# Keys stored for both bands and loaded in one transfer a half; input tiles stored as one run a partition

## The chip, the cores and the metric

The kernel runs on one core of a Trainium2 chip. The metric is the device time of one execution in microseconds; the median of three runs stands for a kernel. A profiled execution supplies the trace: one execution, with its own time.

The core's engines are TensorE (PE, its weight loads PEld), VectorE (DVE), ScalarE (ACT) and GpSimd (POOL). SyncE (SP) here only issues DMA transfers. Each engine has its own in-order instruction stream, and semaphores tie them together. Transfers run on the core's 16 DMA engines.

## The reference

The input is 16 images of 3 x 512 x 512 values in float32. The kernel computes a tokenizer and one transformer layer:

```python
h = patches(x) @ W.T + b                      # 1024 tokens of 256, patches of 3*16*16 = 768
q, k, v = heads(layernorm(h) @ w_qkv)         # 8 heads of 32
k = sum_f a[f]*sin(f*k) + b[f]*cos(f*k)       # f = 1 .. 256, elementwise
h = h + (softmax(q k' * 32**-0.5) @ v) @ w_out + b_out
h = h + shared_mlp(n) + top_2_of_4_experts(n) # n = layernorm(h)
```

The sum of 256 sines and cosines for each element of k is the costly part. Sums are kept in float32.

## The kernel before

The work of an image is cut in two ways. Tokens, projections and networks go by half images (512 tokens). Keys and attention go by head pairs: 4 a image, 64 in all, numbered p.

**Input.** `load_x` (L496 to L505) loads one tile `x` of 128 tokens, 128 partitions x 6 x 128 values, on SP (L501). In HBM an image is laid out as 768 rows of 1024 tokens, so a partition's part of a tile is six pieces of 128 values. There are three buffers; a load is issued when the tile three before it has been used. `tokens` runs the matmuls `tok`.

**Keys.** The angles of k are written to HBM (`ud`, L623). `load_waves` (L971) fetches each row again, spread over partitions, into tiles `w`, eight buffers (two tiles a group g, eight groups a pair); `load_source` (L990) fetches `src` for the tiles `f`. GpSimd multiplies them by frequencies (`turn_waves`, L1026), ScalarE takes the sine (L1036), TensorE mixes (`mix`, `kan`, L1056), VectorE multiplies (L1070), and TensorE adds up (`add_up`, `red`, L1089). After four rounds of `red` a pair's 128 rows of 512 key values stand in PSUM.

`finish_keys` (L1102) splits them into a high part in float32r and the rest (`khi`, `klo`; L635, L636) and writes both to the HBM tensor `kd`, 128 rows of 512 values each (L1108). `stack_keys` (L1114) then fills the two tiles `k4[half]`, named `k` in the profile: 128 partitions x 2 x 512 values of which the first 64 partitions hold the high and low rows (32 each) and the other 64 the same again, so that high and low queries can be multiplied with both. It does this by two transfers of 64 partitions from the same source for each half (L1119), four a pair. Each `kd` transfer writes 256 KB, each `k` transfer loads 256 KB. `stack_queries` (L1136) does the like for queries.

**Attention.** `score` (`sT`, L1155) multiplies keys and queries, ScalarE takes exponentials (`es`, L1170), `weigh` (`av`, L1188) sums values and weights, and VectorE normalizes (L1212 on). Each pair has two attention rounds, over the two halves of the queries, eight scores each; the first four read `k4[0]`, the others `k4[1]`. A pair's keys may be loaded into `k4[half]` after the last score of the pair before that reads it.

**Order.** All loops over images, pairs and groups are unrolled by a planner in the kernel's own source. It keeps a modelled clock for each engine and a queue of steps with dependences (`put`), and lays the next step of SP, POOL, ACT or DVE by modelled readiness. TensorE's order isn't planned: it is a string written out by hand, `ORDER`, one letter a step. `transfer(took, issue)` moves the modelled DMA clock; its result goes into `done[...]`, from which the other steps' due times follow. So a changed number there can move instructions on the planned engines.

After the planned part the kernel checks a flag and, where the softmax sums were out of bounds, would run `general_path`, which this input doesn't reach. It has its own `load_x`.

Of the kernel before, what the change touches and what calls it, by code (L numbers as in the profile page):

```python
# [11 lines left out]
FP = mybir.dt.float32  # L12
# [6 lines left out]
P = 128  # L19
# [3 lines left out]
N = 1024  # L23
NT = N // P
PD = 768
NKC = PD // P
# [17 lines left out]
XT = 128  # L44
# [46 lines left out]
def plain_path(ctx: ExitStack, tc: tile.TileContext, a: dict, out: bass.AP, verdict: bass.AP):  # L91
# [9 lines left out]
    nc = tc.nc  # L101
    xT = a["xT"]
# [3 lines left out]
    def pool(name, bufs, space=None):  # L106
        kw = {} if space is None else {"space": space}
        return ctx.enter_context(tc.tile_pool(name=name, bufs=bufs, **kw))
# [6 lines left out]
    kdp = pool("kdp", 2, DRAM)  # L115
# [137 lines left out]
    k4 = [const.tile([P, 2, 520], FPR, tag=f"k4{i}", name=f"k4{i}") for i in range(2)]  # L253
# [16 lines left out]
    done = {}  # L270
# [8 lines left out]
    def put(engine, queue, cost, deps, key, action):  # L279

        queues[engine].setdefault(queue, []).append((cost, deps, key, action))
# [48 lines left out]
    def transfer(took, issue=0.0, ready=0.0):  # L330

        clock[SP] = max(clock[SP], ready) + issue
        now["dma"] = max(now["dma"], clock[SP]) + took
        return now["dma"] + LANDS
# [161 lines left out]
    def load_x(b, j):  # L496

        b, j = b + j // (N // XT), j % (N // XT)
        if b < B:
            t = xp.tile([P, NKC, XT], FP, tag="x", name="x")  # L500
            nc.sync.dma_start(  # L501
                out=t, in_=xT[b, :, ts(j, XT)].rearrange("(c p) n -> p c n", p=P)
            )
            chunks[b, j] = t
            done["x", b, j] = transfer(1.75, 0.6, clock[PE])  # L505
# [38 lines left out]
    def tokens(b, half):  # L544

        st = images[b]
        if b >= 3:
            yield "written", b - 3, half
        h = st["h", half] = hp.tile([P, 4, E], FP, tag="h", name="h")
        for t in range(4):  # L550
            j = 4 * half + t
            yield "x", b, j
            yield ANY
            ps = side_tile("tok")[:, 0:E]
            for c in range(NKC):
                matmul(
                    out=ps,
                    lhsT=chunks[b, j][:, c, :],
                    rhs=wt[:, c, :],
                    start=(c == 0),  # L560
                    stop=(c == NKC - 1),
                )
            del chunks[b, j]
            load_x(b, j + XBUFS)
            for action in deferred.pop(j + b * (N // XT), ()):
                action()
            yield DVE, 0.41
            nc.vector.tensor_add(h[:, t, :], ps, tokb)  # L568
        mark("tokens", b, half)
# [59 lines left out]
    def split(src, name):  # L629

        hi, lo = (
            rup.tile([P, 512], FPR, tag=tag, name=name + half)
            for tag, half in (("r", "hi"), ("u", "lo"))
        )
        nc.vector.tensor_copy(hi, src)  # L635
        nc.vector.tensor_sub(lo, src, hi.bitcast(FP))  # L636
        return hi.bitcast(FP), lo.bitcast(FP)
# [436 lines left out]
    rows_of_pair = {}  # L1074
# [27 lines left out]
    def finish_keys(p):  # L1102


        def action():
            kd = rows_of_pair["k", p] = kdp.tile([2, P, 512], FP, tag="kd", name="kd")
            for i, x in enumerate(split(rows_of_pair.pop(p), "k")):
                nc.sync.dma_start(out=kd[i], in_=x)  # L1108
            done["kd", p] = transfer(1.4, 1.1, done["keys", p])

        deps = [("red", 4 * p + 3)] + ([("k4", p - 2, 1)] if p > 1 else [])
        put(DVE, "keys", 1.41, deps, ("keys", p), action)

    def stack_keys(p, half):  # L1114

        def action():
            src = rows_of_pair["k", p].rearrange("i (d s h) n -> h (i d) s n", s=2, h=2)[half]
            for j in range(2):
                nc.sync.dma_start(out=k4[half].bitcast(FP)[ts(j, 64), :, 0:512], in_=src)  # L1119
            done["stacked", p, half] = transfer(1.9)  # L1120

        deps = [("kd", p)] + ([("score", 2 * p - 1, 4 * half + 3)] if p > 0 else [])
        put(SP, "keys", 0.8, deps, ("k4", p, half), action)
# [133 lines left out]
    for j in range(XBUFS):  # L1257
        load_x(0, j)
# [73 lines left out]
def general_path(  # L1332
# [33 lines left out]
    nc = tc.nc  # L1366
# [38 lines left out]
    for c in range(2):  # L1405
        for side in range(2):
            nc.sync.dma_start(
                out=wq[:, c, :, ds(64 * side, HD)],
                in_=w_qkv[ts(c, P), 0:E].rearrange(
                    "p (i s d) -> p i s d", s=2, d=HD  # L1410
                )[:, :, side, :],
# [44 lines left out]
    def load_x(b, j):  # L1456
        t = xp.tile([P, NKC, XT], FP, tag="x", name="x")
        nc.gpsimd.dma_start(
            out=t,
            in_=xT[ds(b, 1), :, ts(j, XT)].rearrange("o (c p) n -> p (o c) n", p=P),  # L1460
        )
        return t

# [33 lines left out]
    def stage_tokens(b):  # L1497

        h = hp.tile([P, NT, E], FP, tag="h", name="h")
        for g in range(2):  # L1500
            ps = big_tile("tok").rearrange("p (t e) -> p t e", e=E)
            for k in range(4):
                j, col = divmod((4 * g + k) * P, XT)
                if col == 0:
                    chunk = load_x(b, j)
                for c in range(NKC):
                    nc.tensor.matmul(
                        out=ps[:, k, :],
                        lhsT=chunk[:, c, ds(col, P)],
                        rhs=wt[:, c, :],  # L1510
                        start=(c == 0),
                        stop=(c == NKC - 1),
                    )
            nc.vector.tensor_add(
                h[:, ts(g, 4), :], ps, tokb.unsqueeze(1).to_broadcast([P, 4, E])
            )
# [397 lines left out]
def _patches(x):  # L1914

    b, c, hh, ww = x.shape
    p = 16
    t = x.reshape(b, c, hh // p, p, ww // p, p).transpose(0, 1, 3, 5, 2, 4)
    return np.ascontiguousarray(t.reshape(b, c * p * p, (hh // p) * (ww // p)))


def _kan_layout(kan_a, kan_b):
# [138 lines left out]
```

## Time and profile before

| | before |
|---|---|
| median of 3 runs, us | 3914.31 (3911.86 to 3915.78) |
| the profiled execution, us | 3913.84 |
| its span in the profile, us | 3912.3 |
| TensorE busy, us | 3811.7 |
| ScalarE busy, us | 3264.3 |
| GpSimd busy, us | 3197.1 |
| VectorE busy, us | 2525.4 |
| DMA traffic, MB | 916.53 |
| granted TensorE clock, mean | 0.994 |

The span runs from the first instruction to the last; the time of the execution has some 1.5 us around it. An engine's busy time leaves out waiting, branches and DMA issues. Matmuls overlap, so their ends are modelled. A line such as "POOL w L1026 <- DMA w<-ud: 273.0, 98, 9.6" reads: in front of GpSimd's instruction of line 1026 that writes `w`, the engine stood idle for 273.0 us in total, 98 times, 9.6 us at the longest, and each time the landing of a transfer from `ud` into `w` ended the wait. "SPq" is SP's queue of DMA issues. A packet is the piece of a transfer that one DMA engine moves at a time; here a piece is one contiguous run.

### The profile page before, as it was taken

What the parts mean: (1) busy time and instruction counts of PE and PEld (TensorE: products, weight loads), DVE (VectorE), ACT (ScalarE), POOL (GpSimd) and SP (SyncE); (2) the same over time, 40 slices, a digit from 0 to 9 for tenths busy, and PEclk for the clock granted to TensorE, in tenths of its full rate; (3) what the DMA queues carried; (4) which work ended last, traced back from release to release, by engine and by line L of the source; (5) the groups of instructions that cost most, each with busy time, mean ns of one, the idle gap of its engine ahead of it and who ended that gap; (6) DMA issues with size and microseconds to landing.
All of it is one profiled execution on the core that took longest, in us unless ns stands there. A gap on an engine that the chain in (4) does not pass through costs nothing.

```text
span 3912.3 us, 102935 instructions
## 1 busy us (share of the span) xinstructions
PE 3811.7 (97%) x40337; PEld 1949.1 (50%) x40337; DVE 2525.4 (65%) x4075; ACT 3264.3 (83%) x3939; POOL 3197.1 (82%) x2328
## 2 busy tenths in 40 slices
PE   7899999999999999999999999999999999999998
PEld 4334454554545555455454545545455554544444
DVE  4756757666675766757667575766767667576552
ACT  2788888888888888888888888888888888888983
POOL 3988879788788878879788788878879888888870
PEclk9999999999999999999999999999999999999999
DMA  7997968888788888878888788787878888778760
GB/s 231 283 255 213 278 197 248 256 230 259 214 260 231 233 262 228 259 218 257 243 236 260 211 255 249 225 255 222 267 214 252 258 226 265 223 231 254 213 179 21
DMA packets 589665, 916.53 MB, mean 234 GB/s; under 512 B 60877, under 2 KB 179573, under 8 KB 589173
## 3 DMA queue, kind: packets, MB, share of 16 engines
q1 hardware_dynamic: 588036, 909.40, 80.0%
q8 instruction: 321, 5.26, 0.6%
q14 instruction: 172, 1.40, 0.1%
q10 hardware_dynamic: 1136, 0.47, 0.0%
HBM read 758.64 MB, written 150.99 MB: 233 GB/s over the span
## 4 chain that ended last, share of the span: by engine, by line
PE 70%; ACT 9%; DMA 9%; POOL 4%; DVE 3%; issue 3%; SPq 1%; ACTq 0%; POOLq 0%; DVEq 0%
PE av L1188 17%; PE sT L1155 10%; PE kan L1056 9%; DMA w<-ud 6%; PE red L1089 4%; PE tok L319 4%; ACT w L1036 3%; PE e1p L319 3%; PE e3p L319 3%; PE tok L322 3%; POOL w L1026 2%; ACT f L1036 2%; PE e1p L322 2%; ACT es L1170 2%; PE s1p L319 2%
## 5 line engine op out<-in xcount | busy, mean ns | idle before, releaser
L1026 POOL TENSOR_TENSOR w<-w,lane 128x1024 int32<-128x1024 int32 x1024 | 1925.6, 1897 | 391.6 <-DMA w<-ud 273.0
L1170 ACT ACTIVATE es<-sT 128x1024 f32<-128x1024 f32 x1024 | 1014.9, 1022 | 340.9 <-PE sT L1155 296.8
L1036 ACT ACTIVATE w<-w 128x1024 f32<-128x1024 int32 x1024 | 1013.3, 1046 | 70.5 <-POOL w L1026 67.3
L1026 POOL TENSOR_TENSOR f<-f,lane 128x1024 int32<-128x1024 int32 x512 | 971.4, 1897 | 105.2 <-DVE f L1011 89.8
L1070 DVE TENSOR_TENSOR f<-kan,f 128x1024 f32<-128x1024 f32 x512 | 605.0, 1214 | 207.9 <-ACT f L1036 112.1
L1155 PE MATMUL sT<-q,k 128*128 128x512 f32 x2048 | 708.1, 455 | 22.0 <-ACT es L1170 12.3
L1011 DVE STREAM_SHUFFLE f<-src 128x1024 int32<-128x1024 int32 x512 | 683.1, 1373 | 0.4
L1188 PE MATMUL av<-es,v 128*32 128x256 f32 x8192 | 638.7, 383 | 14.8 <-ACT es L1170 12.3
L1188 PE MATMUL av<-es,ones 128*32 128x256 f32 x8192 | 631.0, 380 | 0.0
L1056 PE MATMUL kan<-w,coef 64*32 64x512 f32 x8192 | 542.3, 599 | 20.5 <-ACT w L1036 13.2
L1036 ACT ACTIVATE f<-f 128x1024 f32<-128x1024 int32 x512 | 518.9, 1045 | 4.2 <-POOL f L1026 4.2
L1155 PEld LDWEIGHTS sT<-q,k 128*128 128x128 f32 x2048 | 350.8, 189 | 316.8 <-issue 137.1
L1188 PEld LDWEIGHTS av<-es,v 128*32 128x32 f32 x8192 | 234.7, 109 | 356.2 <-issue 232.9
L1188 PEld LDWEIGHTS av<-es,ones 128*32 128x32 f32 x8192 | 267.1, 110 | 176.4 <-issue 1.4
L1212 DVE RECIPROCAL rc<-av 128x256 f32<-128x256 f32 x128 | 224.7, 1755 | 164.4 <-PE av L1188 164.3
L1056 PEld LDWEIGHTS kan<-w,coef 64*32 64x32 f32 x8192 | 129.3, 105 | 317.2 <-issue 127.3
L1089 PE MATMUL red<-f,pack 128*32 128x512 f32 x2048 | 271.6, 603 | 0.0
L319 PE MATMUL tok<-wt,x 128*128 128x256 f32 x768 | 182.6, 390 | 18.8 <-DMA x<-in_xT 11.1
L531 ACT ACTIVATE hn<-h,less,rstd 128x256 f32<-128x256 f32 x256 | 140.7, 591 | 52.4 <-POOL less L523 51.8
L1036 ACT ACT_TABLE_LOAD x128 | 164.2, 1283 | 17.8 <-DMA w<-ud 15.5
L322 PE MATMUL tok<-wt,x 128*32 128x256 f32 x3072 | 178.0, 380 | 1.0 <-DVE h L568 1.0
L319 PEld LDWEIGHTS tok<-wt,x 128*128 128x128 f32 x768 | 148.1, 195 | 54.9 <-issue 21.3
(148 smaller groups left out, 4264.5 us busy)
## 6 DMA issues: line engine op xcount, KB each, us to landing
w<-ud SPq DMA_DIRECT2D x2048, 256.0 KB
q<-qd SPq DMA_DIRECT2D x512, 128.0 KB
k<-kd SPq DMA_DIRECT2D x256, 256.0 KB
x<-in_xT SPq DMA_DIRECT2D x128, 384.0 KB
ud<-u SPq DMA_DIRECT2D x64, 512.0 KB
ud<-ui SPq DMA_DIRECT2D x64, 512.0 KB
src<-ud SPq DMA_DIRECT2D x512, 64.0 KB
qd<-qhi SPq DMA_DIRECT2D x64, 256.0 KB
```

Source lines behind the costliest of these rows:

```text
L319: nc.tensor.matmul(out=out, lhsT=lhsT, rhs=rhs, start=start, stop=stop)
L322: nc.tensor.matmul(out=out[ts(i, 32)], lhsT=lhsT[:, ts(i, 32)], rhs=rhs, start=start, stop=stop)
L1011: nc.vector.stream_shuffle(w, sources[g // 8].rearrange("p r n -> p (r n)"), [4 * (g % 8) + i // 8 for i in range(32)],)
L1026: nc.gpsimd.tensor_tensor(w, w, f.to_broadcast([P, N]), ALU.mult)
L1036: nc.scalar.activation(x, w, AF.Sin, scale=TURN * 2.0**-32)
L1056: nc.tensor.matmul(out=ps[ds(64 * j + 32 * blk, 32), ts(r, 512)], lhsT=coef[ts(r, 64)].rearrange("p e f j -> p (e f j)"), rhs=w[ts(r, 64), ...
L1070: nc.vector.tensor_mul(w, kan.pop(g), w)
L1089: nc.tensor.matmul(out=rows_of_pair[p][ts(2 * i + r, 32), :], lhsT=pack[:, ds(PACK0 - 16 * (k % 2) - 2 * (k // 2), 32)], rhs=prod[:, ts(r, ...
L1155: nc.tensor.matmul(out=ps[:, ts(s, 512)], lhsT=k4[kc // 4][:, s, ts(kc % 4, P)], rhs=q4[:, s, :], start=True, stop=True,)
L1170: nc.scalar.activation(es, scores.pop(kc), AF.Exp, scale=SCALE)
L1188: nc.tensor.matmul(out=acc[0][ts(i, HD), ts(half, 256)], lhsT=ones32 if half else v[:, kc, p % NPAIR, ts(i % 2, HD)], rhs=es[:, ds(512 * ( ...
L1212: nc.vector.reciprocal(rc[0], acc[0][:, 256:512])
```

## The change

Two things change.

The input is laid out anew before the launch: (image, token tile, partition, 6, 128) instead of (image, 768, 1024). A partition's part of a tile is then one run of 768 values. Both `load_x` follow.

`kd` gets a leading dimension of two. Each of the two writes of `finish_keys` stores its 128 rows twice, once for either half of the partitions of `k4`, from a source repeated with stride zero. The rows for `k4[half]` are then 128 in number, at one stride, and `stack_keys` loads them in one transfer of 128 partitions, 512 KB. The waits that tie these transfers to each other stay. The planner's figure for the load goes from 1.9 to 1.4; that for the write stays.

```diff
 def load_x(b, j):
             nc.sync.dma_start(
-                out=t, in_=xT[b, :, ts(j, XT)].rearrange("(c p) n -> p c n", p=P)
+                out=t, in_=xT[b, j]
             )
 ...
 def finish_keys(p):
-            kd = rows_of_pair["k", p] = kdp.tile([2, P, 512], FP, tag="kd", name="kd")
+            kd = rows_of_pair["k", p] = kdp.tile([2, 2, P, 512], FP, tag="kd", name="kd")
             for i, x in enumerate(split(rows_of_pair.pop(p), "k")):
-                nc.sync.dma_start(out=kd[i], in_=x)
+                nc.sync.dma_start(
+                    out=kd[:, i].rearrange("j p n -> p j n"),
+                    in_=x.unsqueeze(1).to_broadcast([P, 2, 512]),
+                )
 ...
 def stack_keys(p, half):
-            src = rows_of_pair["k", p].rearrange("i (d s h) n -> h (i d) s n", s=2, h=2)[half]
-            for j in range(2):
-                nc.sync.dma_start(out=k4[half].bitcast(FP)[ts(j, 64), :, 0:512], in_=src)
-            done["stacked", p, half] = transfer(1.9)
+            src = rows_of_pair["k", p].rearrange("j i (d s h) n -> h (j i d) s n", s=2, h=2)
+            nc.sync.dma_start(out=k4[half].bitcast(FP)[:, :, 0:512], in_=src[half])
+            done["stacked", p, half] = transfer(1.4)
 ...
 def _patches(x):
-    return np.ascontiguousarray(t.reshape(b, c * p * p, (hh // p) * (ww // p)))
+    t = t.reshape(b, NKC, P, N // XT, XT).transpose(0, 3, 2, 1, 4)
+    return np.ascontiguousarray(t)
```

## The prediction

> **What bounds the kernel now.** I read the page first, then the waits of TensorE and of SP's queue, then stretches, then the trace's DMA packets.
>
> ```profile
> span 3912.3 us, 102935 instructions
> PE 3811.7 (97%) x40337; PEld 1949.1 (50%) x40337; DVE 2525.4 (65%) x4075; ACT 3264.3 (83%) x3939; POOL 3197.1 (82%) x2328
> q1 hardware_dynamic: 588036, 909.40, 80.0%
> ```
>
> TensorE is idle for 3912.3 - 3811.7 = 100.6 us. That caps what any edit off TensorE can give, apart from small gaps inside "busy". SP's DMA queue keeps the 16 DMA engines busy for 80% of the span, so it is the resource next in line. The waits of TensorE in the first 500 us:
>
> ```profile
> PE kan L1056 <- ACT w L1036: 13.2, 11, 3.3
> PE tok L319 <- DMA x<-in_xT: 11.1, 1, 11.1
> PE sT L1155 <- DVE f L1070: 5.7, 9, 2.2
> ```
>
> None of them names k<-kd, and x is named once: the first token tile. All else waits for DMA only through others (w lands, GpSimd turns, ScalarE takes the sine, then kan). Stretches cut at the first score of an image (columns: length, then busy time of PE, PEld, DVE, ACT, POOL, clock, DMA share, GB/s):
>
> ```profile
> 0.00:154.20 154.20, 119.18 (x761) 65.60 (x761) 88.93 (x149) 60.50 (x81) 94.68 (x88) 0.90 0.81 243
> 154.20:359.30 205.10, 194.07 (x2224) 79.50 (x2224) 120.36 (x173) 181.10 (x202) 183.38 (x104) 0.98 0.89 253
> 359.30:601.50 242.20, 231.62 (x2487) 115.27 (x2479) 159.11 (x252) 205.41 (x248) 199.62 (x144) 0.99 0.79 233
> 1549.70:1786.00 236.30, 234.25 (x2519) 122.15 (x2518) 156.98 (x255) 203.44 (x246) 199.63 (x145) 1.00 0.84 241
> ```
>
> The first 601.5 us hold 56.6 us of the idle time (35.0 + 11.0 + 10.6). A steady image takes 236 us with 2.0 us idle. Hidden slack is of like size: taking, at each of the 2518 places of the matmul order, the second shortest interval over ten like images, an image would take 233.8 us, where those ten took 235.0 to 238.3. So a steady image has some 2 us to give, and only the part that DMA causes.
>
> SP's own waits and a stretch of its queue show where the edited transfers stand:
>
> ```profile
> SPq L971 <- PE kan L1056: 182.0, 102, 9.0
> SPq L1119 <- DMA kd<-klo: 121.1, 60, 4.8
> ```
>
> ```profile
> 1713.13 0.34 SPq L1108 DMA_DIRECT2D kd<-khi  x1
> 1713.86 0.34 SPq L1108 DMA_DIRECT2D kd<-klo  x1
> 1716.02 2.48 SPq L1119 DMA_DIRECT2D k<-kd  x4
> 1718.61 11.17 SPq L971 DMA_DIRECT2D w<-ud  x14
> ```
>
> SP is blocked until kd has landed (2.0 us a pair), issues four k loads at 0.6 us each, and only then the w loads on which GpSimd lives.
>
> **Service times.** I gave the trace's packets to the transfers in order of issue and, where the queue was full, took the time from the end of one transfer to the end of the next (medians). For 256 KB: kd 0.77 us, ud 0.69 (1.38 for 512 KB), w 0.91, k 1.14. An x packet of 512 bytes takes 27 ns in the median, 31 in the mean, so an x tile 768 x 31 / 16 = 1.5 us; an x tile alone spreads over 2.0 us. The 1024-byte packets take 46 ns, the 2048-byte packets of kd 85, those of k 133.
>
> **What the Trainium skill says.** "SBUF — State Buffer", section "Door 1: The DMA port swizzle", says that partitions 0 to 63 reach only 8 of the 16 ports, and 64 to 127 the other 8. The trace agrees in direction: k, 64 partitions a transfer, is the slowest row (1.14 us). "DMA: Bandwidth & Descriptors", section "Rules for kernel authors", says that two transfers to disjoint partition halves serialize and advises one of 128 partitions; the trace has each k transfer's data begin as the one before ends. The same page, "Why small descriptors are slow (HBM only)", gives each packet a fixed overhead; the trace shows 27 ns for 512 bytes and 46 for 1024, so about 8 ns a packet. Its section "Two DMAs through the same engine are not ordered" is why the k load must keep its wait for kd; the 121.1 us above are its price.
>
> **The change, part by part.**
>
> *x laid out in runs.* 768 packets of 512 bytes become 128 of 3072 bytes a tile. From the 1024-byte row a 3072-byte packet costs about 3 x 46 = 138 ns, so a tile 128 x 138 / 16 = 1.1 us: 0.4 less. Bounds: nothing (w's rate, 0.91 us for 256 KB, gives 1.37 against the median packet's 1.30) to 0.9 (the 2.0 us spread less 1.1). I take 0.4; x 128 = 51 us of DMA service, nearly all of it beside a busy TensorE. On the path: (a) the first x. Its data ends at 10.0 us, 1.6 after wt's, and TensorE starts at 11.1. Those 1.6 become 1.1: gain 0.5 (0 to 1.5). (b) The fill from 60 to 360 us, where the DMA share is 0.9 or more and the chain runs through landings of 7 to 10 us that are mostly queue: 13 tiles were issued there, 13 x 0.4 = 5 us less queue. The TensorE waits there follow w, so I count half: 2.5.
>
> *kd written twice.* Per pair 512 KB more to HBM: two transfers grow from 0.69 to 1.38 us, +1.4 us of service, and klo lands 1.4 us later. That wait has SP behind it, with everything that it would issue: k, then w, x, q.
>
> *k in one transfer a half.* The half's data, 2 x 1.14 = 2.28 us, becomes one transfer of 128 partitions. Not in the trace; nearest rows are w's rate (1.82 us), the 1024-byte loads (1.47), and ud's writes (1.38). I take 1.5, so a pair saves 1.6 us of service; bounds 0 (the cause is the row pattern in HBM, not the partitions) and 1.8. Issues fall from four to two: with 0.6 us each SP saves 1.2 us (0.8 if one costs 0.8; 1.6 at ud's 0.38).
>
> Sum for a pair: k issue starts 1.4 later and ends 1.4 - 1.2 = 0.2 later; the last k data ends 1.4 - 1.6 = 0.2 earlier where the queue is full. Where SP's issuing sets the pace (k0's issue to k1's data end is 6.0 us now), it ends about 0.4 later. The first half lands about 0.6 later; the first score follows that data by 2.4 us at least (median 7.0), so the score doesn't wait. Hence w behind it starts within 0.4 us of before, and SP often waits there for a buffer anyway (the 182.0 us). Cost: nothing. If that cover is gone, it is 1.4 us a pair (rival below).
>
> *Order.* The planner is told 1.4 for 1.9. Comparing the built programs, TensorE, VectorE and SP keep their order; ScalarE differs in two places, GpSimd in four, where one turn of 1.90 us changes place with a small operation (layernorm or gate). TensorE's slots are fixed; I take 0, bounds -4 to +4.
>
> *Steady images.* Net DMA service over the run: -51 (x) + 64 x (1.4 - 1.6) = -64 us, 1.6% of the span. A queue shorter by 5 us an image trims the late w loads that end in the 2 us of stalls. I count 0.3 us an image over 13 images: 4 (0 to 26, if all 2 us go).
>
> *Sum.* 0.5 + 2.5 + 4 = 7; five pairs' k stand in the full queue of the fill ahead of w and x, 5 x 0.2 = 1; and SP's issuing, 1.2 us shorter a pair, is on the chain of the fill at times: 1. Total -9. The profiled execution took 3913.84 us (span 3912.3 and 1.5 around it), 0.5 under the runs' median of 3914.31. 3913.8 - 9 = **3905 us**, -0.24% of the median.
>
> **Rivals.** *Hidden:* TensorE's fixed work absorbs it. For: 97% busy, no wait of TensorE on k, one on x. Then only the head and a little of the fill show: 3913.8 - 0.5 - 2 = 3911.
> *Slower: SP's wait on kd takes the place of what k gave.* If k's rate comes from its rows in HBM and stays at 2.28 us a half, nothing pays for kd's 1.4 us; break-even is 2.28 - 0.7 = 1.58 us a half. Place: w behind k. Price: the nine pairs up to 601.5 us in full (9 x 1.4 = 13), and one pair of each of the 13 steady images, the one whose w loads end in the 1.0 us stall of TensorE (1666.65), 1.4 x 13 = 18, less x's 7: +24, 3938. Against: w and kd, on 128 partitions, are faster on the same queue.
> *Large gain:* DMA causes all of the steady stalls: 26 and 10 of the fill, 36 less, 3913.8 - 36 = 3878. Against: the stalls of steady images name ScalarE's exponentials and VectorE, not DMA.
>
> **How the numbers follow.** About 0.2% (7.8 us) is what a measurement of this kernel tells from no change. Forecast case, 3890 to 3906: 0.47; hidden, 3907 to 3921, its own 3911 and the forecast's weak end: 0.31; slower, 3922 to 3945: 0.15; large gain: 0.07. So faster 0.54, same 0.31, slower 0.15. The range 3889 to 3923 leaves out the large gain and most of the slower case. The forecast's own range is 3895 to 3911.
>
> **What would show it.** Right: the packets fall by 81920 for x less 16384 more for kd; DMA share near 78%; k<-kd x128 at 512 KB; the first TensorE wait on x near 10.6 us (11.1 now); the SP wait on kd-klo up from 121 by some 60 to 90 us and still no wait of TensorE on k; the first 601.5 us shorter by 5 or so. Wrong: k's packets still near 133 ns; w waits of GpSimd (273 us) grown; a steady image at 237 or more.

## The result and the profile after

The changed kernel takes 3923.45 us (median of 7 runs, 3918.09 to 3931.7), the kernel before in the same series 3911.86. The ratio is 1.0033, 95% interval 1.0022 to 1.0043: a loss of 0.33%, where the prediction had a gain of 0.24%. The profiled execution of the changed kernel took 3919.52 us.

The page of the changed kernel:

```profile
span 3918.0 us, 102791 instructions
...
PE 3808.3 (97%) x40337; PEld 1949.8 (50%) x40337; DVE 2532.9 (65%) x4075; ACT 3262.7 (83%) x3939; POOL 3194.2 (82%) x2328
...
q1 hardware_dynamic: 520452, 942.94, 79.6%
```

TensorE's busy time hardly moved (3811.7 before), and the span grew by 5.7 us: the loss is idle time of TensorE. The two profiled executions lie 5.7 us apart where the medians lie 11.6, so the traces show about half of the loss. SP's queue moved 33.5 MB more in 67,584 fewer packets, at nearly the same share of the DMA engines (80.0% before).

The waits of the changed kernel (engine and line that waited, what ended it, us in total, times, longest), first TensorE's in the first 500 us, then all that the prediction had named and one more:

```profile
PE kan L1056 <- ACT w L1036: 12.8, 12, 3.3
PE tok L319 <- DMA x<-in_xT: 10.6, 1, 10.6
```

```profile
POOL w L1026 <- DMA w<-ud: 291.7, 94, 9.6
...
SPq L1121 <- DMA kd<-klo: 189.9, 63, 5.3
SPq L971 <- PE kan L1056: 184.7, 97, 10.5
...
ACT hn L531 <- POOL less L523: 63.0, 42, 10.6
```

The first x comes 0.5 us sooner, and SP's wait for kd is 68.8 us longer; both were forecast. New is that GpSimd waits 18.7 us longer for w (273.0 before), and ScalarE 11.2 us longer for GpSimd's `less`. Before:

```profile
ACT hn L531 <- POOL less L523: 51.8, 35, 10.6
```

The stretches of the changed kernel, cut at the first score of an image as before (length, busy time of PE, PEld, DVE, ACT, POOL, clock, DMA share, GB/s):

```profile
0.00:153.75 153.75, 116.29 (x760) 65.07 (x761) 88.72 (x149) 60.38 (x81) 94.53 (x88) 0.93 0.83 250
153.75:356.17 202.42, 191.60 (x2224) 79.02 (x2224) 120.22 (x173) 181.22 (x202) 183.38 (x105) 1.00 0.90 268
356.17:600.66 244.49, 233.54 (x2486) 115.95 (x2479) 159.03 (x252) 204.87 (x248) 199.46 (x144) 0.99 0.77 236
1551.08:1789.34 238.26, 234.92 (x2521) 122.28 (x2519) 155.76 (x255) 203.07 (x247) 200.40 (x145) 1.00 0.83 250
```

The first two stretches are 3.1 us shorter together (356.17 for 359.30), the third 2.3 longer (244.49 for 242.20), so at 600 us the changed kernel is 0.8 ahead. From there to the end it loses 6.5. Not all of the 3.1 us need come from the change: up to 356 us the granted clock is higher in this execution (0.93 and 1.00 for 0.90 and 0.98 before), which is 10.2 us of lost clock for 18.8. Images 4 to 13 take 236.62 us in the mean, 236.12 before and 235.52 with the input layout alone (below).

**Where in an image.** TensorE's order is fixed, so ten images of several kernels can be laid over each other: for each of the 2518 neighbouring pairs of matmuls I took the interval above the 10th percentile over all images and kernels. Summed by 8 us of the image (from its first score), the excess is the same for all within about 0.3 us, except at 32 to 40 us: 0.14 us before, 0.10 with the input layout alone, 0.73 in the changed kernel. That place in one image of the changed kernel (timelines of GpSimd, ScalarE and TensorE: start, length, engine, line; in brackets the idle time ahead and what ended it):

```profile
1105.51 1.89 POOL L1026 TENSOR_TENSOR w<-w,lane 128x1024 int32<-128x1024 int32 x1 [1.00 <-DMA w<-ud]
1107.49 0.23 POOL L519 TENSOR_SCALAR rstd<-mv 128x4 f32<-128x4 f32 x1
...
1109.45 1.09 ACT L531 ACTIVATE hn<-h,less,rstd 128x256 f32<-128x256 f32 x2 [1.71 <-POOL less L523]
1110.45 0.35 ACT L808 ACTIVATE rows<-gate,gb 128x128 f32<-128x128 f32 x1
...
1110.85 0.33 PE L328 MATMUL gateT<-ident,rows 128*128 128x128 f32 x1 [1.32 <-ACT rows L808]
```

The same in the kernel before:

```profile
1105.97 0.23 POOL L519 TENSOR_SCALAR rstd<-mv 128x4 f32<-128x4 f32 x1 [0.39 <-DVE mv L516]
...
1107.94 1.09 ACT L531 ACTIVATE hn<-h,less,rstd 128x256 f32<-128x256 f32 x2 [0.22 <-POOL less L523]
1108.94 0.35 ACT L808 ACTIVATE rows<-gate,gb 128x128 f32<-128x128 f32 x1
...
1110.08 0.27 PE L328 MATMUL gateT<-ident,rows 128*128 128x128 f32 x1
```

Before, GpSimd stands ready and `rstd` waits for VectorE's `mv`. After, GpSimd is still in a turn of w, which itself had waited 1.00 us for its transfer; `rstd` comes behind it in GpSimd's order, `hn` waits for it on ScalarE, `rows` is queued behind `hn`, and TensorE, which wants `rows`, stands for 1.32 us. Three engines pass the delay on, and none of their waits names kd or k.

**What makes GpSimd late.** The keys of the next image's first pair are stored and loaded at the end of each image, with sixteen w transfers and the u stores right behind them. SP's queue there, in the kernel before (image with its first score at 1549.71) and in the changed one (1551.08):

```profile
1534.66 1.09 SPq L1108 DMA_DIRECT2D kd<-khi  x1
1535.85 0.38 SPq L1108 DMA_DIRECT2D kd<-klo  x1
1538.59 2.48 SPq L1119 DMA_DIRECT2D k<-kd  x4
1541.56 3.68 SPq L971 DMA_DIRECT2D w<-ud  x5
```

```profile
1537.12 0.38 SPq L1108 DMA_DIRECT2D kd<-khi  x1
1537.60 0.41 SPq L1108 DMA_DIRECT2D kd<-klo  x1
1541.61 1.23 SPq L1121 DMA_DIRECT2D k<-kd  x2
1542.95 3.46 SPq L971 DMA_DIRECT2D w<-ud  x3
```

From klo's issue to k's is 2.74 us before and 4.01 after; the issues of k shrink from 2.48 to 1.23, so the first w is issued 8.15 us ahead of the first score before and 8.13 after. The w is issued on time, as the prediction had it. But a transfer's data move after those ahead of it in the queue. Packets assigned to transfers in order of issue, in us from the image's first score, medians over the same eleven image ends, those ahead of images 4 to 14:

| | kd issue | kd data end | k issue | k data end | first w issue | its data begin | next u store issue |
|---|---|---|---|---|---|---|---|
| before | -15.04 | -11.45 | -10.85 | -4.97 | -8.14 | -5.09 | 6.82 |
| input layout alone | -15.04 | -11.52 | -11.01 | -5.03 | -8.14 | -5.18 | 6.44 |
| load made wide, kd once | -15.04 | -11.66 | -11.18 | -6.51 | -8.14 | -6.57 | 4.83 |
| changed kernel | -15.04 | -9.98 | -9.54 | -4.38 | -8.13 | -4.47 | 7.39 |

The first w's data begin 0.62 us later, and behind it the queue is full (in the image that begins at 1075.73 us the DMA share of the changed kernel is 0.98 to 1.06 in three stretches from 1072 to 1092 us; 1.03 to 1.10 in the like stretches before), so little is caught up. GpSimd's first turn of that image, before and after:

```profile
1549.20 3.77 POOL L1026 TENSOR_TENSOR w<-w,lane 128x1024 int32<-128x1024 int32 x2 [1.91 <-DMA w<-ud]
```

```profile
1551.75 3.84 POOL L1026 TENSOR_TENSOR w<-w,lane 128x1024 int32<-128x1024 int32 x2 [3.06 <-DMA w<-ud]
```

It starts 0.51 us before the image's first score, and 0.67 after it. Everything in this account up to here is a reading of traces; the experiments test it.

### The profile page after: what moved, and what is told of

It is laid out like the page before. It is cut to its first block, busy times and chain, and to the rows that moved or that the text cites. A ratio compares the mean times of both kernels' runs of the same rounds, so it can differ in the third digit from the quotient of the medians.

```text
span 3918.0 us, 102791 instructions
## 1 busy us (share of the span) xinstructions
PE 3808.3 (97%) x40337; PEld 1949.8 (50%) x40337; DVE 2532.9 (65%) x4075; ACT 3262.7 (83%) x3939; POOL 3194.2 (82%) x2328
## 4 chain that ended last, share of the span: by engine, by line
PE 66%; DMA 13%; ACT 10%; POOL 5%; issue 3%; DVE 2%; SPq 1%; POOLq 0%; ACTq 0%; DVEq 0%
PE av L1190 16%; PE sT L1157 9%; PE kan L1056 9%; DMA w<-ud 8%; PE red L1089 4%; ACT w L1036 3%; PE e1p L319 3%; PE tok L319 3%; POOL w L1026 3%; PE e3p L319 3%; PE tok L322 2%; ACT f L1036 2%; PE e1p L322 2%; ACT es L1172 2%; PE s1p L319 2%
## 5 line engine op out<-in xcount | busy, mean ns | idle before, releaser
L319 PE MATMUL tok<-wt,x 128*128 128x256 f32 x768 | 183.0, 391 | 19.7 <-DMA x<-in_xT 10.6
```

The source lines that it names most:

```text
L319: nc.tensor.matmul(out=out, lhsT=lhsT, rhs=rhs, start=start, stop=stop)
```

## The experiments

All runs are compared with the kernel before on the same chip. The edits are shown in their main lines, "..." for what is left out. The first set parts the change into its pieces.

**x_only**: the kernel before with the edits to `load_x` and `_patches` alone.

```diff
-out=t, in_=xT[b, :, ts(j, XT)].rearrange("(c p) n -> p c n", p=P)
+out=t, in_=xT[b, j]
 ...
```

> The kernel before with the new layout of the input alone. Theory A (the loss comes from the second copy of kd and SP's longer wait for it): faster than before by 2 to 5 us (ratio 0.9987 to 0.9995), the first 360 us some 2 us shorter. Theory B (the 3072-byte packets of x, 170 ns each, hold up the w loads behind them): slower by 3 to 8 us (ratio 1.001 to 1.002). Theory C (the planner's changed order costs it): as A, since the order here is that of before.

Measured 3908.53 us, ratio 0.9995 (0.9987 to 1.0003): at most a small gain. In the mean an x packet of 3072 bytes takes 163.0 ns (169.7 in the changed kernel) where six of 512 bytes took 6 x 31 = 186, so a tile's service falls from 1.5 to 128 x 163.0 / 16 = 1.30 us (1.36). In the median the packet takes 121 ns for 6 x 27 = 162.

**k_only**: the changed kernel with the old input layout.

```diff
-out=t, in_=xT[b, j]
+out=t, in_=xT[b, :, ts(j, XT)].rearrange("(c p) n -> p c n", p=P)
 ...
```

> The changed kernel with the old layout of the input: only kd written twice, one load a half, and the planner's 1.4. Theory A: slower than the changed kernel by what x gave, ratio to before 1.0040 (12 to 20 us). Theory B: about the time of before, ratio 0.9995 to 1.001. Theory C: about the changed kernel's 1.0033.

Measured 3926.36 us, 1.0043 (1.0029 to 1.0057). The loss belongs to the keys' part, and the input layout takes a little of it away.

**write_twice**: the kernel before, with kd written twice; the old four loads read the first copy.

```diff
-kdp.tile([2, P, 512], ...)           ; dma_start(out=kd[i], in_=x)
+kdp.tile([2, 2, P, 512], ...)        ; dma_start(out=kd[:, i]..., in_=x.unsqueeze(1).to_broadcast([P, 2, 512]))
 ...
-src = rows_of_pair["k", p].rearrange(...)[half]
+src = rows_of_pair["k", p][0].rearrange(...)[half]
```

> The kernel before with kd written twice and its second copy never read; loads, issues and order as before. It takes from the change only the longer write and SP's longer wait. Theory A: slower by 15 to 25 us (ratio 1.004 to 1.006), because nothing gives back the 1.4 us a pair; SP's wait on kd-klo at 190 us or more. Theories B and C: within 0.1% of before.

Measured 3929.71 us, 1.0048 (1.0034 to 1.0062). SP's wait for kd is 188.0 us, as in the changed kernel. The second write alone costs what the change loses and more.

**after_plan19**: the changed kernel with the planner's old figure, so the old order.

```diff
-done["stacked", p, half] = transfer(1.4)
+done["stacked", p, half] = transfer(1.9)
```

> The changed kernel with the planner's figure for the k load put back to 1.9, so that GpSimd and ScalarE keep the order of before. Theory C: back to before or below it, ratio 0.9990 to 1.0005. Theories A and B: as the changed kernel, ratio 1.0025 to 1.0040.

Measured 3921.73 us, 1.003 (1.002 to 1.0041): the moved instructions aren't the cause.

**copy_apart**: the second copy goes to a tensor of its own, by two more transfers behind the first two; the loads wait for the first copy alone.

```diff
+kd2 = kdp.tile([2, P, 512], FP, tag="kd2", name="kd2")
+for i, x in enumerate(parts):
+    nc.sync.dma_start(out=kd2[i], in_=x)
```

> The kernel before with the second copy of the keys written to a tensor of its own by two transfers behind the first two; nothing reads it, and the k loads wait for the first copy alone. The DMA traffic is that of write_twice, with two more issues of 0.34 us on SP, but SP's wait on kd doesn't grow. If the loss is SP's longer wait: SP's wait on kd-klo near 120 us and a ratio of 1.000 to 1.0015. If the loss is the DMA time of the second copy, which stands ahead of the w loads either way: ratio 1.003 to 1.005, as write_twice.

Measured 3919.66 us, 1.0019 (1.0012 to 1.0026). SP's wait for kd falls to 60.0 us, while the two extra issues cost SP about 60 us in all. Less of a loss than with one wait for both copies, 1.0048, though the same bytes are written. At the image's end GpSimd's first turn starts at -0.68 us, where it does before. The loss that is left lies mostly ahead of the steady images: its profile is 6.2 us longer than the one before, and 4.1 of these are lost by the first score of image 3 (605.6 us for 601.5).

**load_wide**: kd written once, each half loaded by one transfer of 128 partitions. Each of these transfers fetches the pair's 256 rows once, in order, in place of this half's 128 rows twice, so the scores are made from other keys; only its times are of use.

```diff
-src = ...rearrange("i (d s h) n -> h (i d) s n", s=2, h=2)[half]
-for j in range(2):
-    nc.sync.dma_start(out=k4[half].bitcast(FP)[ts(j, 64), :, 0:512], in_=src)
+src = ...rearrange("i (d s) n -> (i d) s n", s=2)
+nc.sync.dma_start(out=k4[half].bitcast(FP)[:, :, 0:512], in_=src)
```

> The kernel before with kd written once and one load of 128 partitions a half. The load fetches the 128 rows of both halves in place of its own 64 twice, so the scores are computed from wrong keys; sizes and waits are those of the changed kernel's load. It takes the gain of the load alone: k service 1.5 us a half for 2.28, SP 1.2 us a pair less. If that is worth what the service sum says (1.6 us a pair, and the second copy's 1.4 us cost 19 us): faster by 10 to 20 us (ratio 0.995 to 0.9975). If the load's gain is worth the 2 to 4 us by which k_only stands under write_twice: ratio 0.999 to 0.9997.

Measured 3903.11 us, 0.9982 (0.9975 to 0.9989). Two of its waits are shorter than before, where the changed kernel's are longer:

```profile
POOL w L1026 <- DMA w<-ud: 209.5, 80, 10.0
ACT hn L531 <- POOL less L523: 41.8, 29, 10.6
```

GpSimd's wait for w doesn't order the kernels, though. In x_only, which gains next to nothing, it is as short:

```profile
POOL w L1026 <- DMA w<-ud: 214.0, 79, 9.3
```

So a wide load is a gain of 0.18% by itself, and the second write (0.48% in write_twice) costs more than twice as much. Whether the change's own load is worth the 0.18% isn't shown: load_wide reads neighbouring rows, the change every other row, and the data of a pair's keys take 3.6 us here and 3.9 in the changed kernel.

**interleaved** and **interleaved_x**: kd once; the two copies of a row on neighbouring partitions, so that a transfer of 128 partitions can read each row twice, one for each band; queries go to every second partition. The second has the new input layout.

```diff
+for s in range(2):
+    nc.sync.dma_start(out=k4[half].bitcast(FP)[:, s, 0:512],
+        in_=src[:, s, :].unsqueeze(1).to_broadcast([64, 2, 512]))
-out=q4.bitcast(FP)[ds(64 * j + HD * x, HD), :, :],
+out=q4.bitcast(FP)[ds(64 * x + j, HD, step=2), :, :],
```

> The kernel before with kd written once, and k4's partitions laid out so that the two copies of a row are neighbours (partition 2*(32 i + d) + j). A half is loaded by two transfers of 128 partitions from 64 rows, each read twice; the query loads write every second partition of 64 accordingly. No second copy and no longer wait: k near w's 0.91 us for 256 KB in place of 1.14, SP's issues as before. If only the write lost the time: ratio 0.998 to 0.9997. If query loads into every second partition are slower than 0.55 us, or a row read twice is slow: 1.000 to 1.002.

> The same with the new layout of the input as well. x alone measured 0.9995; together 0.9975 to 0.9992 if the two add up, and below both kernels in any case if interleaved is under 1.0005.

Measured 3915.78 us, 1.0014 (1.0005 to 1.0022), and 3915.89, 1.0013 (1.0005 to 1.0021). SP needs 0.64 us to issue a strided q transfer where it needed 0.42, 328 for 214 us in all, and the kd transfers behind the q at the image's end are issued 0.4 to 1.0 us later. The k packets are faster (105 ns in the mean in interleaved, 133 before), but a pair's keys take 4.65 us as before (4.64): four transfers of 128 partitions, each row read twice, are no quicker than four of 64.

**pairs_x**: the same keys, and q loaded into 64 neighbouring partitions at a time.

```diff
+out=q4.bitcast(FP)[ts(x, 64), s, :],
+in_=src[:, ts(s, HD), :].rearrange("j d n -> d j n"),
```

> The new input layout, kd written once, and the two copies of a row put on neighbouring partitions (as in the runs interleaved and interleaved_x), so that a transfer of 128 partitions can read each row twice: two transfers of 256 KB for each half, one a band. Unlike in those runs the queries keep their pace: they are loaded by four transfers of 64 neighbouring partitions (high and low rows paired by the source), one for each band and copy, in place of four into every second partition. Theory A (the loss of the changed kernel comes from the second write; that of the interleaved runs from SyncE's slower issue of the queries): SyncE's q issues stay near 215 us in all (328 when strided), kd's data takes 1.8 us a pair and k's 3.5 to 3.8, and the ratio is 0.9965 to 0.9993, about 3903 us. Rival F (the interleaved runs lost for another reason, the repeated reads): 1.001 or above, with q's issues at 215 us.

Measured 3916.82 us, 1.0012 (1.0005 to 1.0018). Neither theory's condition held: SP's issues of q stayed at 312 us, 0.61 each, though no destination is strided any more. And the keys' data took 4.7 us a pair, no less than before (4.6). The run says nothing about the second write.

**load_again**, **load_again_s**, **load_again_x**: kd once, each row read twice by a stride of zero over the two copies, the copies outermost; load_again_s with two transfers a half, load_again_x with the new input layout.

```diff
+nc.sync.dma_start(out=k4[half].bitcast(FP)[:, :, 0:512],
+    in_=src.unsqueeze(0).to_broadcast([2, 64, 2, 512]))
```

> The kernel before with one edit: each half of the keys is one transfer over 128 partitions that reads every row of kd twice (a stride of 0 over the two copies); kd is written once, as before, and the input has its old layout. Theory A (what costs in the change is the second copy's write, which holds back the keys and, at the end of an image, the sixteen w transfers and the u rows queued right behind them; what gains is the load over 128 partitions): the data of kd takes 1.7 us as before and not 2.8, the data of both halves of k 3.5 to 3.8 us and not 4.6, so the keys of the last pair end about 1.1 us earlier than before, the u store of that place is issued 1 to 2 us earlier against the image's first score, and the time is that of the run with the wide load alone, 3903 us, ratio 0.998 (0.9965 to 0.9992). Rival D (reading one row twice within a transfer is slower than reading two copies, since both reads go to the same place in memory): k takes 4.6 us or more, ratio 1.000 or above.

> As the run that reads each row of kd twice from a kd written once, but with two transfers of 256 KB for each half, one for each band, over all 128 partitions: SyncE issues four transfers a pair as before, and only the number of partitions that one transfer writes is changed. If the gain of the wide load is the partitions (a transfer into 64 partitions is slower), k takes 3.5 to 3.9 us of data for both halves and the ratio is 0.998 to 0.9993, 3904 to 3908 us; if the gain is the two issues that fall away (1.3 us of SyncE a pair), k takes 4.3 to 4.6 us and the ratio is 0.9995 to 1.0005.

> The run with each half of the keys read twice by one transfer from a kd written once, and the input's new layout with it: the whole change but for the second write. Theory A: the second write alone turned the change into a loss, so 3901 us, ratio 0.9975 (0.996 to 0.999), some 2 us under the run without the new layout and some 22 us under the changed kernel. Rival D (one row read twice is slower than two copies): 1.000 or above. Rival E (the new layout and the wide load draw on the same slack and don't add): as the run without the new layout, 3903.

Measured 4897.82 us, 1.2526 (1.2509 to 1.2543); 4922.42, 1.2592 (1.2574 to 1.2609); 4905.35, 1.2531 (1.2514 to 1.2548). All expectations failed. The DMA view of the first, for 10 us in which one k load is under way, and the stretch around it:

```profile
q1 hardware_dynamic: 249, 0.51, 13.1%
...
k<-kd SPq DMA_DIRECT2D x1, 512.0 KB
```

```profile
1300.00:1312.00 12.00, 10.85 (x112) 4.63 (x96) 11.67 (x20) 9.57 (x11) 6.61 (x5) 1.00 0.14 52
```

13.1% of 16 engines are 2.1: such a transfer keeps about two DMA engines busy, at 52 GB/s. The packets themselves are not slow: 13.1% of 16 engines for 10 us, over 249 packets, are 84 ns each (k's took 133 before), and 256 of them on two engines make 10.7 us for one half. It is as if a transfer is dealt out over the engines by its outermost dimension, which is two here.

**paired_x**: kd once, its rows stored so that both bands of a row are one run of 4 KB; each half one transfer that reads every row twice, the 64 rows outermost; high and low queries stored side by side, two q transfers for four; the k tiles without their padding of 8 values; new input layout.

```diff
-nc.sync.dma_start(out=kd[i], in_=x)
+nc.sync.dma_start(out=kd[:, i].rearrange("h d s n -> (d s) h n"), in_=x)
+nc.sync.dma_start(out=k4[half]..., in_=src.unsqueeze(1).to_broadcast([64, 2, 1024]))
```

> The new input layout; kd written once, its rows laid out so that the two bands of a key row stand side by side in HBM; each half of the keys loaded by one transfer of 128 partitions that reads each row of 4 KB twice, for two neighbouring partitions, the 64 rows outermost (in the slow runs the two copies were outermost); the queries stored with high and low rows side by side, so that 64 partitions are filled by one transfer from one contiguous block, two transfers an attention round in place of four. Keys in SBUF are without the padding of 8 values. Theory A: kd's data takes 1.8 us a pair as before, k's 3.5 to 3.8, SyncE issues 128 k and 256 q transfers (80 and 110 to 160 us in all, now 158 and 215), so 0.996 to 0.9985, about 3900 us. Rival D (reading a row twice is slower than two copies, even when all 16 engines take part): k's data takes 4.6 us or more; 0.9995 or above.

Measured 3910.19 us, 0.9999 (0.999 to 1.0007). The keys' data take 3.8 us a pair (median; 4.6 before), so reading a row twice isn't slow in itself, and the two busy engines above belong to the order of the dimensions. The time missed: no gain is left over x_only, though GpSimd's first turn starts at -1.92 us. Part of the load's gain is paid again at the write, which now stores its rows in another order: kd's issues take SP 74.9 us in all for 49.7 in x_only, and SP's wait for kd is longer than in x_only, the second line:

```profile
SPq L1118 <- DMA kd<-klo: 150.1, 60, 5.5
```

```profile
SPq L1119 <- DMA kd<-klo: 118.0, 60, 4.1
```

Whether that is all of it isn't settled.

**The stall at 32 to 40 us.** Two edits of SP's order alone test what makes it; no other engine's order moves.

**after_w_first** and **x_w_first**: in thirteen images the queries of one attention round, not read before 58 us, go behind w transfers that stood behind them (in eleven of the images eight transfers, two groups), among them the ones whose turn stands ahead of `rstd`.

```diff
 deps = [("queries", b, i // 2)] + ...
+if att % 8 == 2 and 24 < att and 4 * att + 8 < total:
+    deps.append(("load", 4 * att + 8, 1))
```

> The changed kernel with one edit to SyncE's order, in twelve steady images: the four query transfers of attention round 8b+2, not needed before 58 us of the image, are issued after the w transfers of two groups that follow them instead of ahead. No other engine's order moves. Theory G (those w land too late in the changed kernel, GpSimd's turn of them stands ahead of the layernorm's rstd, and TensorE stalls behind it at 32 to 40 us of each image): the w lands at 22 to 23 us of the image and not at 24.7, the stall there falls from 0.73 us to 0.1 to 0.2, and the time falls by 12 x 0.6 = 7 us against the changed kernel, ratio to before 1.0015 (1.0005 to 1.0023). Rival H (the stall and the late w only go together; both follow from the keys being late): ratio 1.003 as the changed kernel, and the stall stays at 0.6 or more although the w lands early.

> The kernel before with the new input layout alone, and the same edit to SyncE's order. Theory G: the w lands at 22.5 us there already, below the threshold, so there is nothing to gain: 0.9995 (0.9985 to 1.0005), a stall at 32 to 40 us of 0.1 us. Rival I (the edit helps or harms by itself, through the later queries): more than 0.1% to either side of the run without it.

Measured 3923.51 us, 1.0031 (1.0023 to 1.0039), and 3908.48, 0.9994 (0.9985 to 1.0002). The w landed 2.9 us earlier, yet GpSimd's turn of it started as late as in the changed kernel. Theory G fell: GpSimd was late already, from its first turn of the image on, after which it works nearly without a pause.

**after_k1_later**, **x_k1_later**, **paired_k1_later**: of the last pair loaded ahead of an image, the second half goes behind the first four w transfers, so that GpSimd can start early.

```diff
 deps = [("kd", p)] + ...                                    # stack_keys
+if half == 1 and p % 4 == 0 and 12 <= p < 60:
+    deps.append(("load", 8 * p + 12, 1))
 deps = rows_of(g) + ...                                     # load_waves
+if j == 0 and g % 32 == 13 and 12 <= (g - 13) // 8 < 60:
+    deps.append(("k4", (g - 13) // 8, 1))
```

> The changed kernel with one edit to SyncE's order in twelve steady images: of the last pair whose keys are loaded ahead of an image, the second half's load (not read before 6.2 us of the image) is issued after the first four w transfers that stood behind it. No other engine's order moves. Theory J (the loss in steady images is made where GpSimd waits for those w, and is carried 30 us on to the stall): GpSimd's first turn starts at -1.0 us of the image and not at +0.4, the stall at 32 to 40 us falls from 0.73 to about 0.1 us, and the time falls by 12 x 0.6 = 7 us, ratio 1.0015 (1.0005 to 1.0023). Rival H (stall and late w only go together): the turn starts early, but the stall and the time stay, 1.003.

> The kernel before with the new input layout, and the same edit to SyncE's order. Theory J: GpSimd is not late there (-0.9 us), so an earlier first turn is worth little: 0.9995 (0.9983 to 1.0003). If GpSimd's lateness counts at every size, the turn at -2 us gives up to 0.1 us an image, no more than 0.9990.

> The kernel with contiguous keys and queries, kd written once and the new input layout, and the same edit. Theory J: not late there either (its first turn starts near -0.9 us), 0.9997 (0.9985 to 1.0005), as without the edit.

Measured 3933.15 us, 1.0055 (1.0041 to 1.0069); 3920.5, 1.0025 (1.0013 to 1.0036); 3921.17, 1.0033 (1.0021 to 1.0046). Against the same kernels without the edit, the three lost about 0.2 to 0.35%. GpSimd's first turn did start at -2.1 to -2.4 us, but the later w of `rstd`'s place now came late. In x_k1_later (first score at 1079.90):

```profile
1109.47 1.89 POOL L1028 TENSOR_TENSOR w<-w,lane 128x1024 int32<-128x1024 int32 x1 [1.76 <-DMA w<-ud]
1111.45 0.23 POOL L519 TENSOR_SCALAR rstd<-mv 128x4 f32<-128x4 f32 x1
...
1114.82 0.33 PE L328 MATMUL gateT<-ident,rows 128*128 128x128 f32 x1 [1.11 <-ACT rows L808]
```

The k issue had stood in time in which SP has nothing to do; moved, it stands in the full queue, and the late w lands 2.2 us later than in x_only and 1.5 later than in paired_x; in after_k1_later it was late already and stays so. The misses say more than the hit would have: two ways lead to the same `rstd`, GpSimd's early delay and the late w, and the later of the two decides. Medians over ten images, us from the image's first score (the last two columns are the stall at 32 to 40 us, in the mean, and the ratio):

| | first turn | late w landed | `rstd` starts | stall | ratio |
|---|---|---|---|---|---|
| load_wide | -2.41 | 24.89 | 29.52 | 0.08 | 0.9982 |
| x_w_first | -0.88 | 23.94 | 29.52 | 0.08 | 0.9994 |
| x_only | -1.16 | 24.91 | 29.53 | 0.10 | 0.9995 |
| before | -0.68 | 26.03 | 29.52 | 0.14 | 1 |
| paired_x | -1.92 | 25.88 | 29.51 | 0.15 | 0.9999 |
| copy_apart | -0.68 | 25.42 | 29.53 | 0.20 | 1.0019 |
| after_w_first | 0.63 | 24.20 | 30.09 | 0.47 | 1.0031 |
| write_twice | 0.34 | 27.13 | 30.19 | 0.62 | 1.0048 |
| changed kernel | 0.36 | 27.05 | 30.05 | 0.73 | 1.0033 |
| k_only | 0.02 | 26.56 | 29.94 | 0.99 | 1.0043 |
| after_k1_later | -2.15 | 27.11 | 30.30 | 1.01 | 1.0055 |
| x_k1_later | -2.44 | 27.13 | 30.16 | 1.17 | 1.0025 |

(A landing here is the end of the data; the wait for it ends about 1 us later. Of the runs not in the table, interleaved_x has 29.72 and a stall of 0.50, after_plan19 30.24 and 0.74, pairs_x 30.35 and 0.88, paired_k1_later 30.40 and 1.00, interleaved 30.27 and 1.15.) At 29.5 us `rstd` is set by VectorE's `mv` and the stall is 0.2 us or less. A first turn later than about 0, or a w later than some 26.5, goes with a later `rstd`. x_k1_later makes the second of these in a kernel that had neither, and costs 12 us, about 12 images times the 1.07 us by which its stall grew. after_w_first takes only one of the two away and gains nothing. No run takes both away in the changed kernel.

What is shown: the second write costs the time, and a delay of these w transfers by itself makes the stall. What isn't is the rest of the loss. Of the 1.10 us by which an image of the changed kernel is longer than one of x_only, 0.63 are this stall, so over the ten images it makes 6.3 of the 15.2 us between the two profiles. Another 0.28 an image lie at 216 to 224 us, which I didn't follow, nor the first 600 us, in which the changed kernel loses 3.0 on x_only, nor why copy_apart loses 4.1 there.

## Why the prediction was wrong

**Right.** The bound and the rows forecast from it: TensorE's first wait on x (10.6 forecast, 10.6 measured), SP's wait for kd (60 to 90 us more forecast, 68.8 measured), no wait of TensorE on k, SP's issues of k halved (157.6 to 78.6 us). *Order* at nothing held (after_plan19). The fill of the pipeline gained 3.1 us by 356 us, where its terms (0.5 + 2.5 + 1 + 1) had 5; that may be in part luck, since the granted clock was higher in that execution. x_only gained 1.0 there and k_only 0.8.

**The step that failed is "Sum for a pair", in its last lines: "Hence w behind it starts within 0.4 us of before", "Cost: nothing".** w's issue was within 0.1 us of before. But the cover that the prediction named, SP's waits for a buffer, covers SP's time and not the queue's. The w data start 0.62 us later at the end of an image, where sixteen w follow without a gap and the queue stays full for some 20 us; and there GpSimd, ScalarE's order and TensorE have no slack behind them. The sum itself had two cases, the last k data 0.2 us earlier in a full queue or about 0.4 later where SP's issuing sets the pace. It was the second: from the issue of kd to the last data of k is 10.4 us before and 10.8 after in the median of all pairs, and in steady images each of the four pairs is later, by 0.4 to 0.6. A delay was foreseen, then, and given no price; the pair with the full queue behind it has one.

**Its terms.** *kd written twice*: 1.4 us forecast, measured +1.16 for the data of both transfers in the median pair (1.66 to 2.82), +1.47 to the end of kd's data at the image's end. *k in one transfer a half*: the service was right where a transfer follows another (1.5 us from the end of the first half's data to the end of the second's, forecast 1.5), but the saving of 1.6 a pair was taken from such times, while a pair's k data from first to last took 4.6 before and 3.9 after: 0.7. The first half takes 2.3 us in either kernel, as two transfers or as one, and only the second is short. With 1.2 to 1.5 against 0.7 the pair's balance has the other sign than -0.2. The sum by service assumed a full queue; at an image's end SP issues nothing between kd and k, and k's first data come 1.36 us after their issue in both kernels, in the median pair.

**x laid out in runs**: the old tile, 1.5 us, was priced by the mean of its packets (31 ns), the new one, 1.1, by a median (3 x 46 = 138 ns). Like with like, six packets made one took 121 ns for 162 by the medians, which is the 5 x 8 of the overhead, and 170 for 186 by the means. The gain of 0.4 us a tile was 0.13 by the means and 0.33 by the medians, and *Steady images*, forecast at -4 with the DMA time that x and k would free, didn't come: x alone gave 0.05%, within its interval of nothing. The bound of nothing that the prediction had worked out from w's rate (1.37 us a tile) was near the mean measured (1.36).

**The rival.** "SP's wait on kd takes the place of what k gave" named the place (w behind k, one pair of each steady image) and the sign. Its condition, that k's rate stays at 2.28 us a half, held for the first half alone; the wait decided without the second. Its 3938 us lie some 15 us above the result, the forecast of 3905 lies 18 below. On the line "two transfers to disjoint partition halves serialize", which the prediction drew from the Trainium skill, "DMA: Bandwidth & Descriptors", section "Rules for kernel authors": load_wide's 0.9982 agrees with that advice, though the runs don't part the number of partitions from the number of transfers: in interleaved four transfers of 128 partitions gained nothing on the keys' 4.6 us. What the change pays for its 128 partitions, a second write with a wait on it, is the loss.

## What to carry to other kernels

When a longer wait is paid for by faster transfers after it, add the two up in time from first to last data, not in service time, and do so at the place where the most work is queued behind; an issue that is on time says nothing if the queue ahead of it is late. Follow a delayed transfer to the first in-order engine that has no gap until it meets the bounding engine: here that was GpSimd, for 30 us, and the wait that appeared at its end named only ScalarE. And before moving a transfer out of the way, see whether it stands in idle time now.

## What the runs showed of the hardware

- A transfer whose outermost dimension is two ran on about two of the 16 DMA engines (13.1% of their time, 52 GB/s; load_again). With the 64 rows outermost a pair's keys took 3.8 us, for 4.6 before (paired_x).
- Runs of 3072 bytes read from HBM into the x tiles took 169.7 ns a packet in the mean and 121 in the median, runs of 512 bytes 31 and 27: 18.1 bytes a ns for 16.5 by the means, 25 for 19 by the medians.
- A transfer's issue on SP cost 0.37 us (kd) to 0.67 (src) in the mean before, and not by its bytes: 0.62 for a k transfer of 256 KB and 0.61 for one of 512; q 0.42, but 0.61 to 0.64 with strided destinations or with a source that interleaves two row blocks.
- TensorE's clock was granted at half for windows of 3.41 us, one to three of them in a row and mostly in the first 400 us, in each of these kernels: 23.9 us of clock lost by this before, 16.5 in the changed kernel, 19.5 in x_only, 26.7 in copy_apart. The sums don't order the kernels, but one window, half of 3.41, can shift a single profile by up to 1.7 us.
